# A state-space layer and a gated attention on one core: other places for a few waits, and the last sequence's end in two halves

## The chip, the core and the metric

The kernel runs on one core of a Trainium2 chip, in float32 throughout. A core has TensorE (PE: matmuls and transposes through the identity), VectorE (DVE), ScalarE (ACT), GpSimd (POOL) and SyncE (SP), which issues most of the DMAs; GpSimd issues those that add to memory. The metric is the time of one execution in microseconds (us); lower is better.

## The reference

For each of B=8 sequences of S=512 tokens with D=256 features:

```python
x = x + layernorm(mamba(layernorm(x)))
x = x + layernorm(ffn_block(layernorm(x)))

# mamba: 512 channels, 16 states, convolution of 4 taps
x_ssm, z = split(x @ in_proj_w.T)
xc = silu(conv(x_ssm) + conv_b)
dt_r, Bv, Cv = split(xc @ x_proj_w.T)
dt = softplus(dt_r @ dt_proj_w.T + dt_proj_b)
h[t] = exp(dt * A) * h[t-1] + dt * Bv * xc      # a scan over the tokens
y = sum over states of h * Cv, + xc * D
return (y * silu(z)) @ out_proj_w.T

# ffn_block: 16 heads of 64 features, 8 experts each, 2 of them chosen
q, k = rope(src @ Wq), rope(src @ Wk)
gv, go = top-2 gates, sigmoid(src @ Wsel_v), sigmoid(src @ Wsel_o)
v = sum over experts of gv * (src @ Wv)
o = softmax(q @ k.T / 8) @ v
src = ln(src + sum over heads and experts of (o * go) @ Wo)
return ln(src + relu(src @ W1 + b1) @ W2 + b2)
```

## The kernel before

**Stages.** A sequence b goes through four generators. `front(b)` does layernorm, input projection, convolution and the preparation of dt: ScalarE's Abs, Exp and Ln of `row`, a row of bc_d broadcast to all partitions. `mamba(b)` runs 32 scan steps (four groups of channels by eight pairs of states). A step is, on VectorE, `h = bt * dtx`, a scan with the decays `da` that ScalarE has made one step ahead, and `h * ct`; for sequence 0 the scan reads `ps_u`, made by TensorE. GpSimd's DMAs add the results into `xc` (L566). Then come the gate, the output projection, a norm, a second norm (`xn`), transposes into features (`ps_tr_g`, copied to `xt`) and the logits of the experts (`ps_sel`). `best()` turns logits into the top-2 gates on VectorE (reciprocals, maxima, comparisons; some 0.69 us a row): `best(0)` gives `gv`, the gates of v, and puts the sequence into `state`; `heads(b)` then runs `best(1)` for the gates of the outputs, `gt`, transposes them (`ps_go`, L779), copies them to `go` and stores them in DRAM (`go_d`); then the sequence is in `gated`. `inputs_of[b]` is set as soon as the matmuls of the logits are issued.

**Attention.** The 16 heads go in eight pairs. `Pair.project` makes q and k (`ps_qk`, L810) with weights `wqk` from `wqk_d`, a DRAM copy in which q's weights have been scaled by `later_constants`; `scores` (`ps_s`, L848), a softmax on VectorE and ScalarE, `turn_over` (`ps_pt`, L883), `values` (`ps_v`, L907: all experts; VectorE weighs them, `ve`, and GpSimd sums them into `v`), `attend` (`ps_o`, L937, copied to `o`), `weigh` (`og = o * gb`, where `gb` is a broadcast load from `go_d`, L959) and `add_output` (`ps_a`, L983, summed over all pairs in one bank pair). After a sequence's last pair `feed_forward` adds `xt`, transposes the sum (`ps_acc`, L1012), normalizes, transposes (`ps_tr_f`), applies the two layers (`ps_f`, L1040 and L1062) and two more norms, and stores the result.

**Order.** The order of four engines' instructions is written by hand: `ahead()` interleaves a pair's parts with the sums of the pair before and the projection of the pair after,

```python
for part in (
    "v0", "s0", 0, 1, "v1", "s1", 2, 3, "t0", "s2", "v2", "t1", "s3", following, 4,
    "v3", 5, "t2", 6, "t3", 7,
):
```

where numbers are `add_output(k)` of the pair before and `following` is the projection of the next pair, which for a sequence's last pair is the first of the next sequence. Into this `_Order` mixes everything else by planned costs and due times: a generator yields how long its next part should wait, and that part is issued when TensorE's planned time has come so far (a `Free` wait as soon as due, a plain wait only where VectorE is planned idle). `order_of.run(until)` lets the plan go on until a condition holds. So a changed wait moves instructions in the queues of TensorE, VectorE, ScalarE and GpSimd; each engine then executes its queue in order. SyncE's order is left to the scheduler. All VectorE instructions carry line L175, that of a helper, and are told apart by their tiles.

The mamba of sequence b+1 runs on VectorE, ScalarE and GpSimd beside the attention of sequence b. The last sequence's feed-forward has nothing beside it.

Of the kernel before, what the change touches and what calls it, by code (L numbers as in the profile page):

```python
# [26 lines left out]
F32 = mybir.dt.float32  # L27
AF = mybir.ActivationFunctionType
ALU = mybir.AluOpType
# [3 lines left out]
P = 128  # L33
B, S, D = 8, 512, 256
ND = D // P
NT = S // P
# [3 lines left out]
H, HP, E, F = 16, 64, 8, 1024  # L40
NF = F // P
# [15 lines left out]
NET, FIRST = -9, 0.2  # L57
# [40 lines left out]
class _Order:  # L98
# [11 lines left out]
    def pe(self, us):  # L110
        self.now += us
        self.here = self.now
# [103 lines left out]
def _layers(  # L216
# [3 lines left out]
    nc = tc.nc  # L220
    with ExitStack() as ctx:
        pool = lambda name, bufs, **kw: ctx.enter_context(tc.tile_pool(name=name, bufs=bufs, **kw))
        const = pool("const1", 1)
        wpool = pool("weights", 2)
        seq = pool("seq", 2)
        big = pool("big", 7)
        half = pool("half", 5)
        work = pool("work", 2)
# [37 lines left out]
        def later_constants():  # L266

            nc.sync.dma_start(out=w_sel, in_=wsel)
            nc.sync.dma_start(out=angle[:, :, 0, :], in_=rope)
            half_turn = half.tile([P, P], F32, tag="half", name="half_turn")  # L270
            nc.sync.dma_start(out=half_turn, in_=turn)
            nc.sync.dma_start(out=b1_t, in_=b1)
            nc.sync.dma_start(
                out=rows_t.rearrange("p r d -> p (r d)"),
                in_=rows[:, : 4 * D].to_broadcast([P, 4 * D]),
            )
            yield 8.0


            vector.tensor_reduce(sign, half_turn, AX.X, ALU.add)  # L280
            vector.tensor_scalar(angle[:, 1, 0, :], angle[:, 1, 0, :], sign, None, ALU.mult)

            for i in range(H // 2):
                w = wpool.tile([P, 2, ND, P], F32, tag="wqk", name=f"wqk_s_{i}")
                nc.sync.dma_start(out=w, in_=wqk[i])
                yield 6.0
                while i > 1 and 0 not in state:
                    yield Free(2.0)
                nc.scalar.mul(w[:, 0], w[:, 0], HP**-0.5)
# [25 lines left out]
        def front(b):  # L315
# [127 lines left out]
            nc.sync.dma_start(  # L443
                out=row, in_=bc_d[b][2 * NS : 2 * NS + 1, :].to_broadcast([P, S])
            )
            yield free(1.0)
            if b > 1:
                yield from gate()
            yield free(2.0)
# [4 lines left out]
            for m in range(0, NC, 2):  # L454
                u = tile_for(f"u_{b}_{m}", "og")
                for i in range(2):
                    nc.scalar.activation(u[:, i, :], row, AF.Abs, **step_size(m + i))
                yield free(1.4)
                nc.scalar.activation(u, u, AF.Exp, scale=-1.0)
                us.append(u)  # L460
                yield free(1.1)
            while b == 1 and at["step"] < steps - 1:
                yield Free(0.5)
            for u in us:
# [308 lines left out]
        def heads(b, best, gt):  # L773

            yield from best(1, gt)
            yield Free(1.5)
            ps = banks(f"ps_go_{b}")
            for t in range(NT):
                nc.tensor.transpose(  # L779
                    ps[:, 0, bass.ts(t, P)], gt[:, t].rearrange("p h e -> p (h e)"), ident  # L780
                )
            pe(0.6)
            yield Free(0.05)
            go = half.tile([P, S], F32, tag="half", name=f"go_{b}")
            nc.scalar.copy(go, ps[:, 0, :])
            nc.sync.dma_start(out=go_d[b], in_=go)
            gated.add(b)

        class Pair:
# [3 lines left out]
            def __init__(self, b, pair):  # L793
                self.b, self.pair, self.id = b, pair, f"{b}_{pair}"
                self.xt = inputs_of[b]
                self.p, self.og = {}, {}

                self.done = set()

# [130 lines left out]
            def attend(self):  # L930


                self.need(*((of, t) for of in ("pt", "v") for t in range(NT)))
                po = banks(f"ps_o_{self.id}")
                for t in range(NT):
                    for j in range(2):
                        nc.tensor.matmul(  # L937
                            po[j * HP : j * HP + HP, 0, :], lhsT=self.v[:, j, t, :],
                            rhs=self.pt[:, j, t, :], start=(t == 0), stop=(t == NT - 1),
                        )  # L940
# [12 lines left out]

            def weigh(self, q):

                gb = wpool.tile([P, 2, S], F32, tag="gb", name=f"gb_{self.id}_{q}")
# [7 lines left out]
                og = self.og[q] = work.tile([P, 2, S], F32, tag="og", name=f"og_{self.id}_{q}")  # L964
                vector.tensor_tensor(og, self.o.to_broadcast([P, 2, S]), gb, ALU.mult)

            def add_output(self, k):

                if self.pair == 0 and k == 0:
                    sums[self.b] = psum_a.tile([P, ND, S], F32, tag="sum", name=f"ps_a_{self.b}")  # L970
                pa, q, i = sums[self.b], k // 2, k % 2
                order_of.run(lambda: q in self.og)
                if i == 0:
                    w = self.wo = wpool.tile(
                        [P, 2, D], F32, tag="wo", name=f"wo_{self.id}_{q}"
                    )
# [5 lines left out]
                for c in range(ND):  # L982
                    nc.tensor.matmul(  # L983
                        pa[:, c, :], lhsT=self.wo[:, i, bass.ts(c, P)], rhs=self.og[q][:, i, :],
                        start=(self.pair == 0 and k == 0),
                        stop=(self.pair == H // 2 - 1 and k == E - 1),
                    )
                pe(1.71)
                if i == 1 and q + 2 < E // 2:
                    after(0.05, lambda: self.weigh(q + 2))  # L990

        def feed_forward(b, pa):

# [90 lines left out]
            nc.sync.dma_start(out=out[b].rearrange("(t p) d -> p t d", p=P), in_=z)  # L1084
            finished.add(b)

# [6 lines left out]
        def follow(b, pair):  # L1093

            b, pair = (b, pair + 1) if pair + 1 < H // 2 else (b + 1, 0)
            if b < B:
                order_of.run(lambda: b in (state if b else inputs_of))
                pairs[b, pair] = Pair(b, pair)
                pairs[b, pair].project()

# [13 lines left out]
                    part()  # L1114
                order_of.run()

        last = None
        with tc.manual_schedule(engines=MANUAL):
            first = front(0)
            order_of.start(first, 0, next(first))  # L1120
            order_of.start(mamba(0), 0)
            order_of.start(front(1), FIRST, 9.0)
            first_constants()
            order_of.run(lambda: 0 in scanning)
            order_of.start(later_constants(), NET)
            order_of.run(lambda: 0 in inputs_of)
            pairs = {}
            follow(-1, H // 2 - 1)
            for b in range(B):
# [12 lines left out]
            order_of.run(lambda: not (order_of.queue or order_of.rest))  # L1142


# [81 lines left out]
```

## Time and profile before

| | us |
|---|---|
| three runs | 3694.61, 3695.30, 3702.96 |
| median | 3695.3 |
| profiled execution | 3698.07 |
| its span on the core | 3696.3 |
| busy: TensorE | 3413.1 (92%) |
| busy: VectorE | 3047.2 (82%) |
| busy: ScalarE | 1645.2 (45%) |
| busy: GpSimd | 1681.2 (45%) |

The span runs from the first to the last recorded instruction; 1.8 us of the execution lie around it. The granted clock of TensorE is 0.965 of full speed over the span. In the profile's slices a digit is the busy share in tenths, and PEclk the granted clock in tenths. A timeline row gives start and duration, engine, line, operation, the tiles (out<-in), their shapes and how many instructions of one kind follow each other; the bracket behind it gives the idle time before it on that engine and what ended it. A 512-column matmul appears as two records in the trace. Rows of the largest groups, by TensorE's line: sums `ps_a` 967.1 us, `ps_v` 946.8, `ps_s` 294.2, `ps_pt` 266.7, `ps_o` 248.3.

### The profile page before, as it was taken

The numbers are of one execution on the slowest core, as the hardware profiler recorded it, in microseconds if no ns is written. First come the engines' busy times: TensorE is split into PE (matmuls) and PEld (weight loads), VectorE is DVE, ScalarE is ACT, GpSimd is POOL, SyncE is SP. The second block draws the span as 40 slices with busy tenths as digits, with TensorE's granted clock in tenths as the row PEclk, the third lists the DMA queues.
The fourth block names the chain that finished last, engine by engine and source line by source line (L and its number), as shares of the span: only waits on it lengthen the run. The fifth ranks groups of instructions, "written<-read, shape, count | busy, mean of one in ns | idle before, by whom it ended". The sixth has DMA issues, their size and how long they took to land.

```text
span 3696.3 us, 34548 instructions
## 1 busy us (share of the span) xinstructions
PE 3413.1 (92%) x10956; PEld 1626.4 (44%) x10956; DVE 3047.2 (82%) x3190; ACT 1645.2 (45%) x2798; POOL 1681.2 (45%) x1593
## 2 busy tenths in 40 slices
PE   5768889999999999999999999999999999999996
PEld 3633334444344444444444544434444444445443
DVE  7878998799989898999989998899988998754443
ACT  5524443545543455344544446443653444332331
POOL 1415663354645545454454545355444556232230
PEclk7879999999999999999999999999999999999998
DMA  4937774576866768477755868568765777344431
GB/s 144 196 93 183 174 176 119 149 186 166 195 150 162 179 168 196 121 182 177 199 142 142 201 149 209 138 152 194 183 168 132 179 191 175 99 120 112 111 92 57
DMA packets 285604, 578.48 MB, mean 157 GB/s; under 512 B 37608, under 2 KB 124904, under 8 KB 285424
## 3 DMA queue, kind: packets, MB, share of 16 engines
q1 hardware_dynamic: 204656, 427.33, 40.0%
q0 software_dynamic: 80768, 148.95, 24.1%
q8 instruction: 89, 1.46, 0.2%
q14 instruction: 91, 0.75, 0.1%
HBM read 405.72 MB, written 21.51 MB: 116 GB/s over the span
## 4 chain that ended last, share of the span: by engine, by line
PE 47%; DVE 26%; issue 8%; DMA 7%; ACT 5%; POOL 5%; SPq 0%; DVEq 0%; POOLq 0%; ACTq 0%
PE ps_v L907 14%; PE ps_a L983 12%; DVE h L175 11%; PE ps_qk L810 5%; DMA xc<-h 5%; PE ps_s L848 4%; PE ps_o L937 3%; PE ps_pt L883 3%; DVE ve L175 2%; DVE og L175 2%; DVE low L175 2%; PE ps_f L1040 1%; DVE xs L175 1%; DVE hit L175 1%; POOL ve L923 1%
## 5 line engine op out<-in xcount | busy, mean ns | idle before, releaser
L983 PE MATMUL ps_a<-og,wo 128*128 128x512 f32 x2048 | 967.1, 605 | 32.8 <-DVE og L175 32.5
L907 PE MATMUL ps_v<-wv,xt 128*128 128x512 f32 x2048 | 946.8, 606 | 21.4 <-DVE y L175 13.2
L923 POOL TENSOR_TENSOR ve<-ve 128x512 f32<-128x512 f32 x256 | 425.3, 1661 | 1144.9 <-DVE ve L175 994.7
L863 ACT ACTIVATE p<-ps_s,low 128x512 f32<-128x512 f32 x512 | 347.3, 683 | 723.6 <-DVE low L175 723.1
L566 POOL DMA_DIRECT2D xc<-h x504 | 465.1, 1103 | 384.7 <-DMA xc<-h 174.6
L907 PEld LDWEIGHTS ps_v<-wv,xt 128*128 128x128 f32 x2048 | 385.6, 193 | 544.8 <-issue 484.2
L983 PEld LDWEIGHTS ps_a<-og,wo 128*128 128x128 f32 x2048 | 373.1, 192 | 506.4 <-issue 429.0
L175 DVE TENSOR_TENSOR_SCAN h<-da,h 128x1024 f32<-128x1024 f32 x228 | 541.0, 2373 | 10.2 <-ACT da L503 0.2
L872 ACT ACTIVATE p<-p,total 128x512 f32<-128x512 f32 x512 | 341.5, 714 | 260.8 <-DVE total L175 260.4
L175 DVE TENSOR_TENSOR og<-o,gb 128x1024 f32<-128x1024 f32 x256 | 319.7, 1269 | 130.3 <-ACT o L943 72.4
L175 DVE TENSOR_TENSOR ve<-ps_v,gv 128x1024 f32<-128x1024 f32 x256 | 311.4, 1216 | 126.5 <-PE ps_v L907 99.3
L889 ACT COPY pt<-ps_pt 128x1024 f32<-128x1024 f32 x256 | 256.9, 1005 | 356.5 <-PE ps_pt L883 355.2
L503 ACT ACTIVATE da<-dt,decay 128x511 f32<-128x511 f32 x512 | 339.7, 713 | 104.6 <-DVE h L175 101.8
L175 DVE TENSOR_TENSOR h<-bt,dtx 128x1024 f32<-128x1024 f32 x228 | 321.2, 1409 | 33.7 <-DMA xc<-h 28.6
L175 DVE TENSOR_TENSOR h<-h,ct 128x1024 f32<-128x1024 f32 x256 | 339.1, 1324 | 3.8
L175 DVE TENSOR_REDUCE low<-ps_s 128x2 f32<-128x1024 f32 x256 | 310.4, 1213 | 26.6 <-PE ps_s L848 25.6
L924 POOL TENSOR_TENSOR ve<-ve 128x256 f32<-128x256 f32 x256 | 319.2, 1247 | 20.1
L832 POOL DMA_DIRECT2D qk<-sin x256 | 204.7, 1212 | 264.5 <-DVE qk L175 127.2
L848 PE MATMUL ps_s<-qk 64*128 64x512 f32 x1024 | 294.2, 650 | 23.7 <-ACT p L863 12.8
L883 PEld LDWEIGHTS ps_pt<-ident,p 128*128 128x128 f32 x2048 | 239.5, 141 | 132.0 <-issue 94.8
L937 PE MATMUL ps_o<-pt,v 128*64 128x512 f32 x1024 | 248.3, 611 | 29.0 <-POOL v L925 16.4
L883 PE MATMUL ps_pt<-ident,p 128*128 128x128 f32 x2048 | 266.7, 273 | 7.6 <-ACT p L872 3.3
(134 smaller groups left out, 3340.3 us busy)
## 6 DMA issues: line engine op xcount, KB each, us to landing
gb<-go_d SPq DMA_DIRECT2D x512, 256.0 KB, 4.9
xc<-h POOLq DMA_DIRECT2D x504, 256.0 KB, 5.7
wv<-in_wv_dram SPq DMA_DIRECT2D x128, 512.0 KB, 5.7
wo<-in_wo_dram SPq DMA_DIRECT2D x512, 128.0 KB, 4.0
ct<-bc_d SPq DMA_DIRECT2D x64, 512.0 KB, 5.9
bt<-bc_d SPq DMA_DIRECT2D x57, 512.0 KB, 5.2
wqk<-wqk_d SPq DMA_DIRECT2D x64, 256.0 KB, 2.6
qk<-sin POOLq DMA_DIRECT2D x256, 64.0 KB, 4.7
```

What stands on the lines that cost most here:

```text
L175: return getattr(self.engine, name)(*args, **kw)
L503: nc.scalar.activation(das[k % 2][:, j, 1:S], dt[:, m, 1:S], AF.Exp, scale=decay[:, m, g + j : g + j + 1],)
L566: nc.gpsimd.dma_start(out=xc[:, k % NC, :], in_=hs[k][:, j, :], accum_op=ALU.add)
L848: nc.tensor.matmul(ps[:, j, :], lhsT=self.qk[feats, 0, bass.ts(t, P)], rhs=self.qk[feats, 1, :], start=True, stop=True,)
L863: nc.scalar.activation(p[:, j, :], ps[:, j, :], AF.Exp, bias=low[:, j : j + 1], accum_out=total[:, j : j + 1],)
L872: nc.scalar.mul(p[:, j, :], p[:, j, :], total[:, j : j + 1])
L883: nc.tensor.transpose(pp[:, j, bass.ts(i, P)], self.p[t][:, j, bass.ts(i, P)], ident)
L907: nc.tensor.matmul(ps[:, i, :], lhsT=self.xt[:, c, bass.ts(t + i, P)], rhs=self.wv[:, c, :], start=(c == 0), stop=(c == ND - 1),)
L923: nc.gpsimd.tensor_tensor(ve[:, :, 0:4], ve[:, :, 0:4], ve[:, :, 4:8], ALU.add)
L924: nc.gpsimd.tensor_tensor(ve[:, :, 0:2], ve[:, :, 0:2], ve[:, :, 2:4], ALU.add)
L937: nc.tensor.matmul(po[j * HP : j * HP + HP, 0, :], lhsT=self.v[:, j, t, :], rhs=self.pt[:, j, t, :], start=(t == 0), stop=(t == NT - 1),)
L983: nc.tensor.matmul(pa[:, c, :], lhsT=self.wo[:, i, bass.ts(c, P)], rhs=self.og[q][:, i, :], start=(self.pair == 0 and k == 0), stop=(self. ...
```

## The change

There are six parts.

1. In `front(1)` the waits before ScalarE's Abs and Exp grow from 1.0, 1.4 and 1.1 to 12.0, 3.5 and 3.5, so that these instructions lie among the scan steps of sequence 0.
2. The scaling of q's weights takes a buffer with the tag `w_m` instead of `wqk`, and from the third on waits for sequence 0's `gated` instead of its `state`, now ahead of the load.
3. `heads` waits 4.0 instead of 1.5 before its transposes.
4. `follow` waits for `inputs_of` (logits issued) for every sequence; before, it waited for `state` (gates of v made) for all but sequence 0.
5. In the last sequence the sums `ps_a` are made in two halves of 256 tokens: four matmuls of 256 columns for a k instead of two of 512, and the input `xt` is added by a matmul with the identity instead of on VectorE. The last pair weighs its four `og` at once, with buffers of other tags for the third and fourth.
6. `last_net` takes the place of the last `feed_forward`. Its weights, `x1` and the second bias are loaded from the last sequence's second pair on, into tiles that the mamba no longer uses; then all stages run for one half of the tokens while the other half is a stage behind.

```diff
             for i in range(H // 2):
-                w = wpool.tile([P, 2, ND, P], F32, tag="wqk", name=f"wqk_s_{i}")
+                while i > 1 and 0 not in gated:
+                    yield Free(2.0)
+                w = wpool.tile([P, 2, ND, P], F32, tag="w_m", name=f"wqk_s_{i}")
                 nc.sync.dma_start(out=w, in_=wqk[i])
                 yield 6.0
-                while i > 1 and 0 not in state:
-                    yield Free(2.0)
                 nc.scalar.mul(w[:, 0], w[:, 0], HP**-0.5)
                 nc.sync.dma_start(out=wqk_d[i], in_=w)
...
-            yield free(1.0)
+            yield free(12.0 if b == 1 else 1.0)
...
                     nc.scalar.activation(u[:, i, :], row, AF.Abs, **step_size(m + i))
-                yield free(1.4)
+                yield free(3.5 if b == 1 else 1.4)
                 nc.scalar.activation(u, u, AF.Exp, scale=-1.0)
                 us.append(u)
-                yield free(1.1)
+                yield free(3.5 if b == 1 else 1.1)
...
         def heads(b, best, gt):
 
             yield from best(1, gt)
-            yield Free(1.5)
+            yield Free(4.0)
...
-                for q in range(2):
+                for q in range(E // 2 if self.final else 2):
                     after(0.8 + 0.1 * q, lambda q=q: self.weigh_soon(q))
...
+            def add_half(self, k, g, w):
+                pa = sums[self.b].rearrange("p g (c s) -> p g c s", c=ND)[:, g]
+                if self.pair == 0 and k == 0:
+                    nc.tensor.matmul(
+                        pa, lhsT=ident, rhs=self.xt[:, :, bass.ts(g, S // 2)],
+                        start=True, stop=False,
+                    )
+                    pe(0.86)
+                for c in range(ND):
+                    nc.tensor.matmul(
+                        pa[:, c, :], lhsT=w[:, bass.ts(c, P)],
+                        rhs=self.og[k // 2][:, k % 2, bass.ts(g, S // 2)],
+                        start=False, stop=(self.final and k == E - 1 and c == ND - 1),
+                    )
...
+        def last_net():
+            b = B - 1
+            w_1 = one.tile([P, ND, F], F32, tag="dt", name="w1_last")
+            w_2 = one.tile([P, NF, D], F32, tag="dtx", name="w2_last")
+            w_o = one.tile([P, E // 2, 2, D], F32, tag="xc", name="wo_last")
+            x1 = big.tile([P, NT, D], F32, tag="big", name="x1_last")
...
+            outputs(0, range(E))
+            outputs(1, range(2))
+            nc.scalar.copy(acc[0], pa[:, 0])
+            outputs(1, range(2, 4))
+            to_tokens(0)
+            outputs(1, range(4, E))
+            normed(0, *first)
+            nc.scalar.copy(acc[1], pa[:, 1])
+            features(0)
+            to_tokens(1)
+            hidden(0, 0)
+            normed(1, *first)
+            hidden(0, 4)
+            features(1)
+            for f in range(0, NF, 4):
+                hidden(1, f)
+            for g in range(2):
+                second(g)
...
-                order_of.run(lambda: b in (state if b else inputs_of))
+                order_of.run(lambda: b in inputs_of)
...
+                    if (b, pair) == (B - 1, 1):
+                        next(net)
...
-            for k in range(E):
-                last.add_output(k)
-                order_of.run()
-            order_of.start(feed_forward(B - 1, sums[B - 1]), NET)
-            order_of.run(lambda: not (order_of.queue or order_of.rest))
+            order_of.run(lambda: not order_of.rest)
+            next(net, None)
```

In `last_net`, `outputs` are the last pair's sums of a half, `to_tokens` and `features` the two transposes with their copies, `normed` a norm with the rows behind it, `hidden` four feature groups of the first layer (256 columns each, in one pair of banks, then four Relus), and `second` the second layer of a half with its two norms and its store.

More of the change, by code (lines that the diff above doesn't have):

```diff
@@ L796, in __init__ @@
                 self.p, self.og = {}, {}
+                self.final = b == B - 1 and pair == H // 2 - 1
                 self.done = set()
@@ L954, in weigh @@
             def weigh(self, q):
-                gb = wpool.tile([P, 2, S], F32, tag="gb", name=f"gb_{self.id}_{q}")
+                spare = self.final and q > 1
+                of, tag = (work, "ve") if spare else (wpool, "gb")
+                gb = of.tile([P, 2, S], F32, tag=tag, name=f"gb_{self.id}_{q}")
                 for j in range(2):
@@ L963, in weigh @@
                     )
-                og = self.og[q] = work.tile([P, 2, S], F32, tag="og", name=f"og_{self.id}_{q}")
+                og = self.og[q] = work.tile(
+                    [P, 2, S], F32, tag="p" if spare else "og", name=f"og_{self.id}_{q}"
+                )
                 vector.tensor_tensor(og, self.o.to_broadcast([P, 2, S]), gb, ALU.mult)
@@ L981, in add_output @@
                         )
[L982 to L987, printed above, removed]
+                if self.b == B - 1:
+                    for g in range(2):
+                        self.add_half(k, g, self.wo[:, i])
+                else:
+                    for c in range(ND):
+                        nc.tensor.matmul(
+                            pa[:, c, :], lhsT=self.wo[:, i, bass.ts(c, P)], rhs=self.og[q][:, i, :],
+                            start=(self.pair == 0 and k == 0),
+                            stop=(self.pair == H // 2 - 1 and k == E - 1),
+                        )
                 pe(1.71)
@@ L990, in add_output @@
                     after(0.05, lambda: self.weigh(q + 2))
+            def add_half(self, k, g, w):
[4 more added lines that the diff above has]
+                        start=True, stop=False,
+                    )
+                    pe(0.86)
+                for c in range(ND):
+                    nc.tensor.matmul(
+                        pa[:, c, :], lhsT=w[:, bass.ts(c, P)],
+                        rhs=self.og[k // 2][:, k % 2, bass.ts(g, S // 2)],
+                        start=False, stop=(self.final and k == E - 1 and c == ND - 1),
+                    )
         def feed_forward(b, pa):
@@ L1085, in feed_forward, with outputs, to_tokens, normed @@
             finished.add(b)
+        def last_net():
[4 more added lines that the diff above has]
+            x1 = big.tile([P, NT, D], F32, tag="big", name="x1_last")
+            b2 = half.tile([P, 1, D], F32, tag="half", name="b2_last")
+            for j in range(2):
+                nc.sync.dma_start(
+                    out=w_o[j * HP : j * HP + HP],
+                    in_=wo[H - 2 + j].rearrange("(i p) q d -> p q i d", i=2),
+                )
+            nc.sync.dma_start(out=w_1, in_=w1)
+            nc.sync.dma_start(out=w_2, in_=w2)
+            nc.sync.dma_start(out=x1, in_=x1_d[b])
+            nc.sync.dma_start(out=b2[:, 0, :], in_=rows[:, 4 * D :].to_broadcast([P, D]))
+            yield
+            pa = sums[b].rearrange("p g (c s) -> p g c s", c=ND)
+            half_of = lambda name: [
+                big.tile([P, ND, S // 2], F32, tag="big", name=f"{name}_last_{g}") for g in (0, 1)
+            ]
+            wide = [P, NT // 2, D]
+            rows_of = lambda i: rows_t[:, i : i + 1, :].to_broadcast(wide)
+            acc, y, yt = half_of("acc"), half_of("y"), half_of("yt")
+            hid = one.tile([P, NF, S], F32, tag="pt", name="hid_last")
+            def outputs(g, ks):
+                for k in ks:
+                    order_of.run(lambda: k // 2 in last.og)
+                    last.add_half(k, g, w_o[:, k // 2, k % 2])
+                    pe(0.86)
+                    order_of.run()
+            def to_tokens(g):
+                ps = banks("ps_acc_last")[:, 0, :].rearrange("p (t d) -> p t d", d=D)
+                for t in range(NT // 2):
+                    for c in range(ND):
+                        nc.tensor.transpose(
+                            ps[:, t, bass.ts(c, P)], acc[g][:, c, bass.ts(t, P)], ident
+                        )
+                nc.scalar.copy(y[g], ps)
+            def normed(g, *then):
+                for _ in norm(y[g], [y[g][:, t, :] for t in range(NT // 2)]):
+                    pass
+                for a, op in then:
+                    vector.tensor_tensor(y[g], y[g], a, op)
+            def features(g):
+                ps = banks("ps_tr_f_last")
+                for c in range(ND):
+                    for t in range(NT // 2):
+                        nc.tensor.transpose(
+                            ps[:, c, bass.ts(t, P)], y[g][:, t, bass.ts(c, P)], ident
+                        )
+                nc.scalar.copy(yt[g], ps[:, :, : S // 2])
+                vector.tensor_tensor(y[g], y[g], b2.to_broadcast(wide), ALU.add)
+            def hidden(g, f):
+                ps = banks("ps_f1_last").rearrange("p a (i s) -> p (a i) s", s=S // 2)
+                for i in range(4):
+                    for c in range(ND):
+                        nc.tensor.matmul(
+                            ps[:, i, :], lhsT=w_1[:, c, bass.ts(f + i, P)], rhs=yt[g][:, c, :],
+                            start=(c == 0), stop=(c == ND - 1),
+                        )
+                for i in range(4):
+                    nc.scalar.activation(
+                        hid[:, f + i, bass.ts(g, S // 2)], ps[:, i, :], AF.Relu,
+                        bias=b1_t[:, f + i : f + i + 1],
+                    )
+            def second(g):
+                ps = banks("ps_f2_last")[:, 0, :].rearrange("p (t d) -> p t d", d=D)
+                for t in range(NT // 2):
+                    for f in range(NF):
+                        nc.tensor.matmul(
+                            ps[:, t, :], lhsT=hid[:, f, bass.ts(g * NT // 2 + t, P)],
+                            rhs=w_2[:, f, :], start=(f == 0), stop=(f == NF - 1),
+                        )
+                vector.tensor_tensor(y[g], y[g], ps, ALU.add)
+                normed(g, (rows_of(2), ALU.mult), (rows_of(3), ALU.add))
+                tiles = slice(g * NT // 2, (g + 1) * NT // 2)
+                normed(g, (x1[:, tiles, :], ALU.add))
+                nc.sync.dma_start(
+                    out=out[b].rearrange("(t p) d -> p t d", p=P)[:, tiles, :], in_=y[g]
+                )
+            first = ((rows_of(0), ALU.mult), (rows_of(1), ALU.add))
+            outputs(0, range(E))
[14 more added lines that the diff above has]
+                hidden(1, f)
+            for g in range(2):
+                second(g)
@@ L1115, in ahead @@
                 order_of.run()
-        last = None
+        last, net = None, last_net()
         with tc.manual_schedule(engines=MANUAL):
```

## The prediction

> **What bounds the kernel now.** I read the page's busy shares and slices first, then the costliest groups, then the start, the sequence boundaries and the end in TensorE's and VectorE's timelines, and last the chain of waits through the end.
>
> ```profile
> PE 3413.1 (92%) x10956; PEld 1626.4 (44%) x10956; DVE 3047.2 (82%) x3190; ACT 1645.2 (45%) x2798; POOL 1681.2 (45%) x1593
> PE   5768889999999999999999999999999999999996
> PEclk7879999999999999999999999999999999999998
> ```
>
> TensorE is the bound: 92% busy, and 129.60 of 129.60 us in the window 3445.90 to 3575.50 (three pairs of heads at 43.2 us each). Nothing in such a stretch gets shorter unless TensorE's work does. Time can be won only where TensorE idles or its clock is low: the first 300 us, the last 81 us, and short gaps inside, at the changes from one sequence to the next. Here is sequence 3's, in TensorE's timeline (start, duration, idle before and releaser), then VectorE's rows of the same place:
>
> ```profile
> 1553.87 3.67 PE L937 MATMUL ps_o<-pt,v 128*64 128x512 f32 x6 [5.68 <-POOL v L925]
> 1559.37 1.11 PE L779 MATMUL ps_go<-ident,gt 128*128 128x128 f32 x4 [1.82 <-DVE gt L175]
> 1560.27 4.59 PE L907 MATMUL ps_v<-wv,xt 128*128 128x512 f32 x8
> ```
>
> ```profile
> 1540.88 3.38 DVE L175 RECIPROCAL s<-s 128x128 f32<-128x128 f32 x4
> 1548.89 1.22 DVE L175 TENSOR_TENSOR ve<-ps_v,gv 128x1024 f32<-128x1024 f32 x1
> 1558.62 0.69 DVE L175 TENSOR_TENSOR gt<-gt,hit 128x512 f32<-128x512 f32 x1
> ```
>
> The last ve of sequence 2 stands on VectorE behind reciprocals, sin and qk of sequence 3, so ps_o waits 5.68; ps_go then waits 1.82 for gt. Both stretch what follows: the granted clock is 0.80 in 1545 to 1570, and the rows beside cost 3.67, 1.11 and 4.59 where a place without a wait (287 to 293) has 1.93, 0.66 and 3.60. Loss at b=3: 5.68 + 1.82 + 1.74 + 0.45 + 0.99 = 10.7 us. The same sum gives 9.5 at b=2 and 12.2 at b=5. At b=4 and b=6 only ps_go waits (3.57 and 3.56, with v at 5.3), 5.3 each. Together 43.0; b=1 and b=7 show no such wait.
>
> The end, in the chain of waits (start, us, what):
>
> ```profile
> 3617.23 3.71 PE ps_a L983 x8
> 3621.64 2.84 DMA wo<-in_wo_dram
> 3624.61 7.21 PE ps_a L983 x16
> ...
> 3642.92 1.95 PE ps_tr_f L300 x8
> 3644.89 1.02 ACT yt L1027
> ...
> 3645.96 9.73 PE ps_f L1040 x16
> 3655.69 7.24 PE ps_f L1062 x32
> 3662.93 6.87 PE ps_f L1040 x16
> 3669.79 7.25 PE ps_f L1062 x32
> 3677.07 1.23 DVE y L175
> ```
>
> Everything is serial: from the last attention sum (3615.3) to the end (3696.3) are 81.0 us, with TensorE busy 48.7.
>
> **The change part by part.** The profiled execution took 3698.1 (span 3696.3 and 1.8 around it), 2.8 above the median 3695.3. The sum is made against it; the forecast then takes the 2.8 off.
>
> *Abs and Exp of sequence 1 (L446, L458, L461).* ScalarE waits 3.88 for row and then runs u ops of 1.52, 1.06 and 1.50 ahead of da; the scan at 123.10 waits 3.13 for that da. Spread over some eight scan steps, each u op fits into ScalarE's slack of a step. Two later scans (175.26, 189.65) wait 2.71 and 3.93 for DMA xc<-h, which issues from POOL behind the scans and may give part back. Between 0 and -3.1; I take -2.0.
>
> *Scaled weights.* Pair 1's projection waits for its weights:
>
> ```profile
> 272.26 5.25 PE L810 MATMUL ps_qk<-xt,wqk 128*128 128x512 f32 x8 [5.51 <-DMA wqk<-wqk_d]
> ```
>
> SyncE issues this load only at 269.48, behind loads and stores of the scaled weights, which hold the two buffers of its tag. With a tag of their own, and with the scaling of weights 2 to 7 put behind sequence 0's go, the loads for pairs 0 and 1 stand early in SyncE's order. That removes 5.51, and 5.25 may become 3.63. The scaling moves into pair 1's softmax on ScalarE, with a store and a load of 256 KB for each weight; ScalarE is 45% busy, so I put it at nothing (uncovered, six rows of at most 0.59: 3.5). Between -7.1 and -2; with the next item -3.6.
>
> *Heads later (1.5 to 4.0) for b=0.* The transposes move behind one ps_v, so go, and with it the gb loads that ps_a at 300.27 (idle 6.21) waits for, come up to 3.6 later; ScalarE's copy by some 1.9. I charge 1.9 of the gain above.
>
> *q and k after the logits, heads later, b=2 to 7.* The new order has ve_(b-1)_7_3 ahead of most of the gating's rows, and ps_go 11 to 14 instructions later at b=2 and 3, where gt (1.82 late) is long done. b=2 keeps about 0.5 of 9.5, b=3 about 0.7 of 10.7: -9.0 and -10.0. From b=4 on there is a price. Logits, q and k follow directly on the last scores of the old sequence in TensorE's queue; before, the transposes ps_tr_g stood 12 to 16 instructions ahead of them. Everything of TensorE queues behind them: four v matmul groups, three turn-overs, the sums. At b=5, VectorE has after ps_s_4_7_3: low 1.21, three BN pairs of 0.6, ln_rs 0.18, h times ct 1.32 (which hides POOL's power of 1.05), xn 1.39. That is 5.9, less the 0.3 or so that the first BN has a start: 5.6 of idle at ps_tr_g, 1.1 for the copy xt, and some 1.3 of low clock after it, by b=3's rows. At b=4 only the last xn row, the low and the power are left: 1.5 + 1.1. b=6 is like b=4. Also, go now stands directly before ps_o_b_0, and the first gb of the sequence needs go copied (0.6), stored (2.4), loaded (4.9) and multiplied (1.2), 9.1 to 11 by whether the issues queue (I take 10.6), against ps_o, the ps_a rest, ps_v and ps_s (3.58 + 0.87 + 3.43 + 1.06 = 8.9): 1.7 late. So b=4 keeps 4.3 of 5.3, b=5 9.7 of 12.2, b=6 4.3 of 5.3: -1.0, -2.5, -1.0. All boundaries: -23.5, between 0 (each wait only changes its name) and -37 (b=4 to 6 lose only the 1.7).
>
> *The last sequence's sums by halves.* A 512-column matmul record costs 1.72/4 = 0.430 (ps_a x4), a 256-column one 7.25/32 = 0.2266 (L1062 x32, at full clock). Per k: 8 x 0.2266 - 4 x 0.430 = +0.093. In seven pairs of eight k: +5.2; adding the input by identity, four records of 0.43, +1.7. Pair 7 is in the end's sum. Cost +6.9, in a stretch where TensorE is 100% busy and nothing hides it; at least 1.7.
>
> The Trainium skill speaks against narrower matmuls too, more mildly: "TensorE: Matmul & The Clock Gate", section Back-to-back issue gap, gives each matmul a fixed 2.5 ns beside its columns. By it the halves would cost an estimated 0.6 for 224 further records, not 5.2; the measured row is the better price, being this kernel's shape.
>
> *The end by halves.* Counted from 3615.3 by the rows above: four og in a row to 3620.7, weights already there (the 3.7 for wo gone). Half 0's sums, 32 records of 0.2266, end 3624.5, half 1's with transposes between at 3632.2. Norm 0 (half the BN, power, multiply and add: some 5 on VectorE) is done at 3633.6, so TensorE idles 1.4 where it idled 8.71. First layer of half 0, 7.25, to 3642.0; the second half's features wait 1.6; then 7.25 to 3651.4, twice 7.25 for the second layer to 3665.9. The last chain has half the rows of 3677.07 to 3692.0 but the same two powers: 8.8, to 3674.7; the output's DMA 4.1 (4.3 before, for twice the size). End 3678.8 against 3696.3: -17.5; -14 if the clock stays low (9.73 instead of 6.87 in one of the four groups). The preloads (3.6 MB of weights and inputs, from pair 1 on) have SyncE's queue ahead of gb and wo loads; DMA is 41% busy there, I charge nothing; a queue blocked for a tile would cost each pair a wait like 2.84.
>
> Sum: -2.0 - 3.6 - 23.5 + 6.9 - 17.5 = -39.7. 3698.1 - 39.7 - 2.8 = 3655.6; as the b=4 to 7 waits were read off an order and not off a trace, I put the forecast 2.4 higher: 3658. Ends: -3.1 - 5.2 - 37 + 1.7 - 17.5 = -61 and 0 + 0 + 0 + 6.9 - 14 = -7; they are unlikely all at once, and the likeliest case's own range is 3640 to 3678.
>
> The same page's section What's actually happening says that TensorE's clock halves after an idle window of about 3.4 us. Row 1553.87 (3.67 for 1.93 after 5.68 idle) agrees; at 640.24 a ps_qk took 5.40 for 3.63 after 1.23 idle alone, which does not. By the page, b=4 and b=6 lose no clock and b=5 does, as in the sum.
>
> **The rivals.** *Boundaries trade waits.* If VectorE, 82% busy and with LEAST gaps in its order, brings xn as late as it brought v, the 23.5 vanish: 3658 + 23.5 = 3682. For it: ps_tr_g waited 13.40 at 221.46 (sequence 0). Against: at b=2 and 3 the old order's row is seen to be late for its place only.
> *Boundaries all clear.* If xn is early, b=4 to 6 gain the 13 that separate 37 from 23.5: 3645.
> *Slower: q and k block the queue.* In the old order q and k came after state, when all was there. Now TensorE, in order, stops at ps_tr_g, ps_sel or ps_qk with ps_o, ps_v and ps_a of the old sequence ready behind. It is slower than before by 11 when the waits at b=4 to 7 exceed my values by (37 + 11)/4 = 12 each, nearly the 13.40 of the first sequence: 3706 or more. VectorE's rows before xn (5.9) speak against it.
> *Halves buy nothing.* If narrow matmuls and six powers instead of three eat 10 of the 17.5, the time is 3668, inside the range; that the change does nothing is excluded by the new order.
>
> **How the numbers follow.** Forecast 0.62; boundaries trade waits 0.17; all clear 0.11; slower 0.10. A measurement of this kernel tells 0.3%, 11 us, from no change: 3684 is the border, and half of the trade case lies above it. Faster 0.62 + 0.11 + 0.09 = 0.82, same 0.08, slower 0.10. The range 3637 to 3690 takes in the clear and the trade case and leaves out the slower one and the ends.
>
> **What would show it.** After, ps_qk of pair 1 has no DMA wait; no ps_o near 1120, 1540 and 2390 waits for POOL v over 1 us; ps_tr_g at b=4 to 6 waits 1 to 6; from the last attention sum to the end are some 64 us; ps_a's last-sequence records are 0.2266. I am wrong if ps_tr_g, ps_sel or ps_qk of b=4 to 7 wait 10 or more, if periods from go to go exceed 428, or if a preload stands between gb loads and TensorE's ps_a.

## The result, and the profile after

The changed kernel is slower: 3734.6 us (median of 3732.28, 3733.98, 3735.28 and 3742.39) against 3696.9 for the kernel before in the same session. The ratio is 1.0105, with a 95% interval of 1.0089 to 1.0121. I had forecast 3658, between 3637 and 3690, with 0.82 on faster. The profiled execution is the longest of the four (3742.4, span 3740.2), some 8 us above the median, so that single rows are read from it and totals from the medians.

The page's first lines, with the same columns as before:

```profile
PE 3418.4 (91%) x11248; PEld 1683.5 (45%) x11248; DVE 3049.8 (82%) x3198; ACT 1653.1 (44%) x2816; POOL 1672.5 (45%) x1596
PE   5768889999899999999998999989999899999997
PEclk7878999999999999999999999999999999999999
```

The work is the same (TensorE is busy 5 us longer), and the span grew by 44: the time went into idling, and it went there in the middle (the 8s), not at the ends. The group of the attention sums says where; here it is in the page before and in the page after (busy us and mean ns, then the idle time ahead of it and its releaser):

```profile
L983 PE MATMUL ps_a<-og,wo 128*128 128x512 f32 x2048 | 967.1, 605 | 32.8 <-DVE og L175 32.5
```

```profile
L993 PE MATMUL ps_a<-og,wo 128*128 128x512 f32 x1792 | 855.9, 611 | 82.7 <-DVE og L175 80.7
```

The group before has the last sequence's sums in it as well; even so, after the change 48 us more are spent waiting for og. The place that I had shown, sequence 3's beginning, is clear, as forecast:

```profile
1548.54 3.65 PE L939 MATMUL ps_o<-pt,v 128*64 128x512 f32 x16
1552.12 3.70 PE L909 MATMUL ps_v<-wv,xt 128*128 128x512 f32 x8
...
1576.06 0.66 PE L779 MATMUL ps_go<-ident,gt 128*128 128x128 f32 x4
```

No bracket, no wait: ps_o runs through, and ps_go, a dozen instructions later, finds gt long done. The granted clock in 1545 to 1570 is 1.00 where it was 0.80. Sequence 4's beginning, in TensorE's timeline, shows the price:

```profile
1966.92 0.77 PE L300 MATMUL ps_tr_g<-ident,xn 128*128 128x128 f32 x5 [1.12 <-DVE xn L175]
1968.98 5.28 PE L712 MATMUL ps_sel<-w_sel,xt 128*128 128x256 f32 x16 [1.30 <-ACT xt L705]
...
2033.31 0.60 PE L779 MATMUL ps_go<-ident,gt 128*128 128x128 f32 x4
2033.84 3.65 PE L939 MATMUL ps_o<-pt,v 128*64 128x512 f32 x16
...
2054.50 5.18 PE L993 MATMUL ps_a<-og,wo 128*128 128x512 f32 x8 [11.48 <-DVE og L175]
```

The waits ahead of the logits are the small ones I had counted. The large one is the last: 11.48 at the first sum of the new sequence (7.70 at b=5, 12.25 at b=6), for which I had put 1.7. Followed backwards through ScalarE's, SyncE's and VectorE's timelines:

```profile
2037.54 0.59 ACT L945 COPY o<-ps_o 128x512 f32<-128x512 f32 x1 [4.59 <-PE ps_o L939]
2038.02 0.59 ACT L785 COPY go<-ps_go 128x512 f32<-128x512 f32 x1
```

```profile
2036.51 0.76 SPq L1025 DMA_DIRECT2D w<-in_w_dram  x1
2037.36 1.76 SPq L984 DMA_DIRECT2D wo<-in_wo_dram  x2
2039.17 1.72 SPq L1057 DMA_DIRECT2D b<-in_rows_dram  x1
2040.98 0.69 SPq L786 DMA_DIRECT2D go_d<-go  x1
2048.22 1.75 SPq L963 DMA_DIRECT2D gb<-go_d  x3
```

```profile
2053.22 1.23 DVE L175 TENSOR_TENSOR og<-o,gb 128x1024 f32<-128x1024 f32 x1 [12.46 <-DMA gb<-go_d]
```

ps_go is done at 2033.9. ScalarE copies it at 2038.0, because its queue has the copy of o first and that waits for ps_o. SyncE stores it at 2041.0, behind the loads of w, wo and b. The first gb load is issued 7.2 later, and og can start 5.0 after that: 19.9 us from ps_go's start to og's, where the four rows of TensorE beside it (ps_o to ps_s) cover 9.2. The load's issue waits until the store has landed: at b=6, where the trace holds the landing, the store landed at 2934.89 and the load was issued at 2934.90. In the kernel before, the first gb load of b=4 was issued at 2001.7, 33 us ahead of its og at 2034.9, so that none of this showed.

The end, in the chain of waits, is shorter (the rows up to the second layer):

```profile
3674.03 10.60 PE ps_a L1013 x40
...
3685.29 1.99 PE ps_a L1013 x8
...
3694.21 7.19 PE ps_f_last L1179 x32
...
3703.52 7.17 PE ps_f_last L1179 x32
3710.69 6.92 PE ps_f_last L1193 x32
```

From the last attend (3672.1) to the end (3740.2) are 68.1 us, against 81.0.

### The profile page after: what moved, and what is told of

Same layout as the page of the kernel before. It is cut to its first block, busy times and chain, and to the rows that moved or that the text cites. A ratio compares the mean times of both kernels' runs of the same rounds, so it can differ in the third digit from the quotient of the medians.

```text
span 3740.2 us, 35144 instructions
## 1 busy us (share of the span) xinstructions
PE 3418.4 (91%) x11248; PEld 1683.5 (45%) x11248; DVE 3049.8 (82%) x3198; ACT 1653.1 (44%) x2816; POOL 1672.5 (45%) x1596
## 4 chain that ended last, share of the span: by engine, by line
PE 43%; DVE 26%; DMA 9%; issue 8%; ACT 6%; POOL 5%; SPq 0%; DVEq 0%; POOLq 0%; ACTq 0%
PE ps_v L909 12%; DVE h L175 9%; PE ps_a L993 9%; PE ps_qk L812 5%; DMA xc<-h 5%; PE ps_s L850 3%; DVE og L175 3%; PE ps_o L939 3%; PE ps_a L1013 3%; DVE low L175 3%; DVE ve L175 3%; PE ps_pt L885 2%; DMA gb<-go_d 2%; POOL ve L925 1%; PE ps_out L676 1%
## 5 line engine op out<-in xcount | busy, mean ns | idle before, releaser
L925 POOL TENSOR_TENSOR ve<-ve 128x512 f32<-128x512 f32 x256 | 413.3, 1614 | 1189.7 <-DVE ve L175 1072.5
L993 PE MATMUL ps_a<-og,wo 128*128 128x512 f32 x1792 | 855.9, 611 | 82.7 <-DVE og L175 80.7
L993 PEld LDWEIGHTS ps_a<-og,wo 128*128 128x128 f32 x1792 | 330.0, 194 | 499.5 <-issue 370.0
L812 PE MATMUL ps_qk<-xt,wqk 128*128 128x512 f32 x512 | 240.7, 614 | 16.3 <-DVE ve L175 9.3
```

Of the source, the lines that this page charges most:

```text
L812: nc.tensor.matmul(ps[:, i, :], lhsT=w[:, i, c, :], rhs=self.xt[:, c, :], start=(c == 0), stop=(c == ND - 1),)
L925: nc.gpsimd.tensor_tensor(ve[:, :, 0:4], ve[:, :, 0:4], ve[:, :, 4:8], ALU.add)
L993: nc.tensor.matmul(pa[:, c, :], lhsT=self.wo[:, i, bass.ts(c, P)], rhs=self.og[q][:, i, :], start=(self.pair == 0 and k == 0), stop=(self. ...
```

## The experiments

Two theories stood at first. A: part 4 (q and k wait for logits only) lets all that VectorE does for the next sequence slip back against TensorE's queue, so that go comes too late. B: part 3 (the longer wait of heads) makes go late.

**Part 4 undone**, the rest kept.

```diff
-                order_of.run(lambda: b in inputs_of)
+                order_of.run(lambda: b in (state if b else inputs_of))
```

> The changed kernel with part 4 undone: follow waits for state again, for all but sequence 0; heads keep 4.0. Theory A (the place of q and k, part 4, lets everything that VectorE does for the next sequence slip about 17 instructions back in TensorE's queue; go, its store and the gb loads then come too late): the waits of 11.5, 7.7, 12.3 and 5 us before ps_a at b=4 to 7 go, ps_tr_g waits no longer at the end of a sequence, and what stays is the start (-6) and the end (-13) against before's 3697: 3678, or down to 3670 if one place more for ps_go also takes its 1.8 to 3.6 us waits for gt away. Theory B (the longer wait of heads makes go late): only ps_tr_g's waits of some 3, 7 and 3 and their low clock go: 3715 to 3722.

3681.6 us, ratio to before 0.9964 (0.9951 to 0.9977). As A said: one condition in the planner's loop is worth 53 us. The waits for og at the first sums of b=4 to 6 are gone. (The 5 us that the expectation puts at b=7 stand inside sequence 6, at 3109 in the changed kernel's trace.)

**Part 3 undone**, the rest kept.

```diff
             yield from best(1, gt)
-            yield Free(4.0)
+            yield Free(1.5)
```

> The changed kernel with part 3 undone: heads wait 1.5 again; ps_go then stands 2 instructions ahead of where the change has it at b=4 to 7, b=3 4 ahead. Theory A: each of the four late go comes some 2.6 us earlier on TensorE and its copy perhaps 4 us earlier on ScalarE (in front of the o copy): -4 to -6 a boundary, 3735 - 20 = 3715 (3708 to 3725). Theory B: the 37 us of og waits at b=4 to 7 go nearly whole: 3690 to 3700.

3734.8 us, 1.0112 (1.0095 to 1.0129): no difference to the changed kernel. B falls. A's size of 20 us falls too: in the trace the waits for og at b=4 to 6 are shorter (8.9, 4.9 and 6.7, in sum by 11), but there are new ones, of 4.0 for og at b=3 and of 10.3 for pt in sequence 2.

**Part 4 alone**, in the kernel before.

> The kernel before with part 4 alone. Theory A: it makes nearly the whole loss: 3735 + 6 (start) + 13 (end) - 20 (go two instructions earlier, as above) = 3734, between 3725 and 3755. Theory B: q and k behind the logits alone cost only ps_tr_g's waits and save the waits for v: 3690 to 3705.

3750.0 us, 1.015 (1.0135 to 1.0165): A's number. Part 4 by itself makes the whole loss.

**Parts 3 and 4 undone**, which leaves start and end.

> The changed kernel with parts 3 and 4 undone: what is left is the start (1, 2) and the end by halves (5, 6). Both theories: 3697 - 6 - 13 = 3678 (3672 to 3684), with before's waits at b=2 to 6 as they were. If the start's 6 us are given back later, as sequence 1's part of the trace hints (its pairs 1 to 7 take 5 us longer), 3684.

3676.8 us, 0.9955 (0.9941 to 0.9968). Start and end together bring 16.6 us (0.0045 of 3697).

**The chain shortened.** The changed kernel with go copied directly behind its transposes, and stored from ScalarE's DMA queue:

```diff
             pe(0.6)
-            yield Free(0.05)
             go = half.tile([P, S], F32, tag="half", name=f"go_{b}")
             nc.scalar.copy(go, ps[:, 0, :])
-            nc.sync.dma_start(out=go_d[b], in_=go)
+            nc.scalar.dma_start(out=go_d[b], in_=go)
```

> The changed kernel (3735) with two edits in heads: ScalarE's copy of go is placed directly behind the transposes (ahead of the copy of o, which waits for ps_o), and its store is issued from ScalarE's DMA queue, not from SyncE's, where at b=4 it came behind loads of w, wo and the bias. TensorE's order stays as in the changed kernel. Theory A1 (the chain go, store, gb, og is what costs most at b=4 to 6): 4.1 for the copy and 1 to 2.4 for the issue come off each of the waits of 11.5, 7.7 and 12.3: -15 to -20, 3715 to 3720. Theory A2 (the waits behind ps_tr_g and the low clock carry it, and the chain's wait is only a part that moves elsewhere, as the heads' 1.5 made it 2 to 6 shorter without a change in time): 3728 to 3736.

3727.6 us, 1.0077 (1.0062 to 1.0092): 7 us better by the medians, less than A1 and near A2. Its ScalarE and SyncE rows tell why A1 was too high:

```profile
2033.14 0.58 ACT L784 COPY go<-ps_go 128x512 f32<-128x512 f32 x1 [0.99 <-PE ps_go L779]
2033.75 0.33 ACTq L785 DMA_DIRECT2D go_d<-go  x1
```

```profile
2041.81 1.78 SPq L962 DMA_DIRECT2D gb<-go_d  x3
```

Counted from ps_go, the store is issued 6.4 us earlier, but the gb issue then comes 8.1 behind it, and og 7.8 behind that, so that og gains 2.8. The store and the gb loads run among the loads of bt, ct, w and wo (the DMA engines are busy 0.78 of the time in 2030 to 2060 of the changed kernel, 0.38 in 1980 to 1996); that this crowd is what makes them slow is likely, but no run isolates it. The three waits fell to 8.7, 6.4 and 8.7, in sum by 7.6, about the time gained.

**The chain cut.** The changed kernel in its own order, where the first pair's gb loads of b=4 to 7 read the stored gates of the sequence before (so that pair's gates are another sequence's):

```diff
-                        in_=go_d[self.b][r : r + 2, :]
+                        in_=go_d[self.b - (self.b > 3 and self.pair == 0)][r : r + 2, :]
```

> The changed kernel (3735), its order untouched, with one operand replaced: at b=4 to 7 the first pair's gb loads read the go_d of the sequence before (long stored), so that nothing there waits for go (the output gates of that pair are those of another sequence). If the chain go, store, gb, og is the cost that I had put at 1.7 a boundary: the waits of ps_a at the second pair of b=4 to 6 (11.5, 7.7, 12.3) fall to 0 to 3, with 1 to 3 us of low clock behind each: -30 to -36, 3699 to 3705. If other late work (tr_g's wait, acc, the norm of the feed-forward) only takes the place: 3720 to 3735.

3699.3 us, 1.0019 (1.0007 to 1.0031): 35 us below the changed kernel, as the theory had it. TensorE at sequence 4's beginning:

```profile
2018.74 0.60 PE L779 MATMUL ps_go<-ident,gt 128*128 128x128 f32 x4
2019.28 3.65 PE L939 MATMUL ps_o<-pt,v 128*64 128x512 f32 x16
...
2028.38 3.70 PE L993 MATMUL ps_a<-og,wo 128*128 128x512 f32 x8
```

The sum follows without a bracket. So 35 of the 58 us between the changed kernel and the one with start and end alone are this chain (by the ratios, 32 of 55). The other 23 are not. The edit does one thing more: with nothing to wait for, SyncE issues the first gb load at 1990.7, 28 us ahead of ps_go, so that these loads leave the crowded place as well.

**The plan's wait behind q and k.** The changed kernel, with the wait for the gates put directly behind the projection:

```diff
                 pairs[b, pair].project()
+                order_of.run(lambda: b in state or not b)
```

> The changed kernel with one line more: follow projects q and k as soon as the logits are issued, and then the planner waits for state, before any further part of the pair (before, it waited ahead of the projection; in the changed kernel it waits only behind the next sequence's first v). q and k are still ahead of the gates in VectorE's order. Theory A (what counts is the place in TensorE's order at which the plan waits for VectorE): the loss goes, ps_tr_g stands 12 instructions ahead of the last scores again, 3672 to 3682. Rival C (q and k ahead of the gates' rows delay gv, gt and go on VectorE): 3715 to 3735.

3732.1 us, 1.0097 (1.0078 to 1.0116). My theory of the place of the wait falls here. ps_tr_g and ps_go are back where they were and wait no more, and the time is lost elsewhere: from the last ps_o of sequence 2 to that of sequence 5, ps_o waits 18.3 for ScalarE's pt (6.1 in the kernel before), 15.2 for POOL v (5.7), and ps_a 15.6 for og (0.7). Rival C's range held, but its mechanism is not shown: ps_go has no wait, and the v that is late is the old sequence's last. What is shown is that the planner's order, once shifted, puts other late work on the path.

**The gates of the outputs later**, in the kernel without part 4, by a planned wait ahead of them (6.0 in the first run, 10.0 in the second):

```diff
+            yield 10.0
             yield from best(1, gt)
             yield Free(4.0)
```

> The first experiment's kernel (changed kernel without part 4, 3680) with a planned wait of 6.0 ahead of the gates of the outputs, so that three of the eight reciprocal rows stand ahead of the old sequence's last ve and the rest behind it; ps_go 16 instead of 19 to 20 instructions ahead of the next ps_o. If the waits of ps_o for POOL v (4.3, 5.7, 5.7 at b=2, 3, 5) come from these reciprocals, they go with some 1.7 to 3 us of low clock each: -15 to -22, 3658 to 3665. If ve waits for sin and qk, or v for GpSimd, 3676 to 3682.

3704.3 us, 1.0018 (1.0008 to 1.0027): slower than without it, and outside what I expected. At each of b=3 to 6 ps_o waits for POOL v (5.29), and in each of sequences 3 to 5 for pt (4.61): the same pattern as in the run before, here without q and k being moved.

> As the one before with 10.0 instead of 6.0: all reciprocals of the outputs' gates stand behind the last ve; ps_go 14 instructions ahead of the next ps_o. Same theory: 3656 to 3665, the waits for POOL v gone, unless go is now late for the gb loads, which the first ps_a of the second pair would show.

3672.4 us, 0.9927 (0.9912 to 0.9942). With all reciprocals behind the last ve the waits for POOL v are gone (0.8 us in three sequences), but a wait of 3.9 at ps_pt and one of 6 at ps_o have come.

**10.0 with part 3 undone as well.**

> The fastest so far (late gates 10.0, 3672) with the heads' wait at 1.5: ps_go stands 15 instead of 14 instructions ahead of the next ps_o, the first sequence's and the second's orders change somewhat. If the order's pattern from b=3 on is what decides, the time stays, 3668 to 3676. If it falls back into the pattern of the planned wait of 6.0 (ps_o behind ScalarE's pt by 4.6 and behind POOL v by 5.3 at each of b=3 to 6), 3695 to 3707.

3697.7 us, 1.001 (0.9998 to 1.0022), a miss, for a reason that I had not thought of: against the run before it loses 25 us by the end of sequence 1 (18 of them in sequence 0) and then nothing up to the end: the pattern from b=3 on stayed, as expected, and the first two sequences' order paid.

**10.0 for sequences 0 to 2 alone.**

```diff
+            yield 10.0 if b <= 2 else 0.0
```

> The kernel of the first experiment (changed kernel without part 4) with the planned wait of 10.0 ahead of the outputs' gates for sequences 0 to 2 alone. TensorE's order is that of the run with 10.0 everywhere up to sequence 2, which at the end of sequence 2 was 13 us ahead of the kernel with start and end alone, and has ps_tr_g 12 and 16 instructions ahead of the last scores in turn from b=3 on, as the kernel before has it, with 426 us a sequence. If a sequence's time from b=3 on is that of its order, the 13 us are kept: 3677 - 13 = 3664 (3658 to 3670). If b=3 pays for it, 3672 to 3678.

3668.5 us, 0.9919 (0.9904 to 0.9934), within the expected range: the fastest version here by the median (the interval overlaps that of 10.0 everywhere), 0.8% ahead of the kernel before and 66 us ahead of the changed one. The 13 us were not all made: by the end of sequence 2 it is 8 us ahead of the run with start and end alone, and a wait of 5.68 for POOL v still stands there; these 8 it keeps (8.6 at the last attend).

**The end alone** (parts 5 and 6 in the kernel before).

> The kernel before with parts 5 and 6 alone (sums of the last sequence and its end by halves). By the trace of the changed kernel the end takes 68.1 instead of 81.0 us after the last attention sum, and the sums by halves cost 0.1 us a pair and 1.8 once: -13 + 2.5 = -10.5, 3684 (3680 to 3688). By my sum for it, -17.5 + 6.9 = -10.6: the same total from other terms. The start (1, 2) is then what the run with start and end has beyond this one: -6, or nothing if it is given back.

3687.6 us, 0.997 (0.996 to 0.9981): 11.1 us of gain, so that the start is worth the remaining 5.5 of 16.6. With some 4 to 5 us of uncertainty in each, that difference is not clear of zero, and no run has the start alone.

## Why the prediction was wrong

**Start: the mechanism was right, the size is not shown.** ps_qk of pair 1 no longer waits for its weights (it runs at 266.87 in 3.70, before at 272.26 in 5.25), and the first sums wait 7.95 for og instead of 6.21, by 1.7 more where I had charged 1.9. I had -5.6 for both items; the difference of the two runs, -5.5, is as near as it is partly by luck, since it is uncertain by some 6.

**End: right in sum, by two errors that cancel.** I had -17.5 and +6.9; measured are -12.9 and +3.1 (from the last ps_o of sequence 6 to that of sequence 7, 371.5 us before and 374.6 in the run with the end alone). The end lost two steps of my chain: half 0's sums ran at a granted clock of 0.84 (3674.0 to 3684.6), though the wait ahead of them was the 1.9 that the kernel before has too, where the clock was 1.00 (3617 to 3632); and VectorE did half 0's last norms until 3726.4, so that half 1's, ready at 3724.5, began 1.9 late. The halves' price came from a misread row. In the last sequence a k takes 1.73 from start to start at 256 columns and 1.72 at 512. The 0.2266 of L1062 is a mean over a row of 32 records (3655.5 to 3662.8) in which four early ones are spaced by 0.26 to 0.32; the other 28 follow each other in 0.216, as the halves do. The rule that I had set aside, the 2.5 ns a matmul of the Trainium skill's "TensorE: Matmul & The Clock Gate", section Back-to-back issue gap, gave an estimated 0.6 for the seven pairs. The five pairs that can be compared took 0.4 longer, 43.29 instead of 43.21 each: the page was nearer than my row. The rest of the 3.1 lies in the sequence's first pairs, with the four records that add the input (2.1) and the preloads.

**The boundaries: this step failed.** By the ends of ps_o, from the end of a sequence's pair 2 to that of the next sequence's (us):

| sequence | 2 | 3 | 4 | 5 | 6 | 7 |
|---|---|---|---|---|---|---|
| before | 449.9 | 426.7 | 430.0 | 426.8 | 426.3 | 394.3 |
| after | 439.2 | 428.7 | 447.1 | 446.7 | 440.6 | 403.2 |
| chain cut | 439.1 | 422.0 | 437.3 | 436.3 | 431.1 | 401.6 |
| change forecast | -9.0 | -10.0 | -1.0 | -2.5 | -1.0 | 0 |
| change measured | -10.7 | +2.0 | +17.1 | +19.9 | +14.2 | +8.9 |

The profiled run of the changed kernel is a long one: at b=3 it has the same program as the run with the chain cut, and 6.7 us more, so that single columns are good to some 7 us. At b=2 the gain came, at b=3 about half of it at best. The waits at ps_tr_g and for xt were what I had worked out: 5.68 and 1.10 at b=5 (forecast 5.6 and 1.1), 3.0 at b=4 (2.6). Two things were wrong.

First, the term "1.7 late" for go, 5 us in sum for b=4 to 6. I had 0.6 + 2.4 + 4.9 + 1.2, rows of an unhurried place, taken as 10.6 against 8.9; at b=4 it was 20.5 against 9.2. In the new order the copy stood behind that of o (+4.1), the store behind loads on SyncE (+2.4), and the next load's issue came 7.2 behind the store's where I had 2.4. Those DMAs were in the order that I had read the 1.7 from; I had asked how long each link takes, and not what stands ahead of it on its queue. This is some 35 us by the medians (31 by the table's columns 4 to 7). The kernel before could have warned me: sequence 0 has the store and the load 2.1 us apart,

```profile
292.24 0.33 SPq L786 DMA_DIRECT2D go_d<-go  x1
...
294.31 9.27 SPq L959 DMA_DIRECT2D gb<-go_d  x8
```

but its table of DMAs, in which the last number is the median time from issue to landing, has more for the same store (of the eight landings two are recorded, 6.5 at b=1 and 4.3 at b=2, and 5.4 is their middle):

```profile
go_d<-go SPq DMA_DIRECT2D x8, 256.0 KB, 5.4
```

The Trainium skill's page "DMA: Bandwidth & Descriptors", section Queues, rings and completion order, says that SyncE's and ScalarE's queues are rings on the same 16 DMA engines, and that on an engine a ring's descriptors are consumed in order; the run with the store on ScalarE's queue agrees with the first part, since with a queue of its own the store still kept the load waiting for 8.1, 6.1 and 5.7 us at b=4 to 6 (7.2, 6.6 and 8.6 on SyncE's), not for 2.1. The second part no run here shows.

Second, I treated the wins and costs as if everything between the boundaries stayed. It did not: in the run with the chain cut, TensorE still idles 63 us from the last ps_o of sequence 2 to that of sequence 5, against 44 in the kernel with start and end alone, and its busy time there is 7 us longer. Some 8 of the 19 are the waits at ps_tr_g and ps_sel, which I had counted; the rest are new ones inside the sequences, less old ones that went, among them 2.7 to 3.5 for og three times, and 6.2 for pt in column 4 of the table. In column 7, where I had forecast nothing, 5.25 of the 8.9 us are one wait for og inside sequence 6 (5.59 in the run with the chain cut, none in the kernel before). My rival "boundaries trade waits" named such a trade, but only for xn, and priced it at the gain. The rival that q and k block the queue had the right sign and the wrong mechanism: the block is at ps_a, behind go, not at ps_tr_g. Of my signs of being wrong, the waits of 10 or more at ps_tr_g, ps_sel or ps_qk did not come; the periods from go to go above 428 did (446.8 and 439.4 from b=4 to 6).

**What stays open** is why the planner's order falls into one pattern or another. Moving q and k with the chain cut or with the wait behind them, or delaying the gates by 6.0, gives some 431 to 439 us a sequence in columns 4 to 6; delaying them by 10.0 gives 428 to 429; the order before has 426 to 430. No experiment here isolates the step of the planner that decides it.

## What to carry to other kernels

When a step moves to just ahead of its use, follow the whole way from it to the use (copy, store, landing, load, product), and for each link look at what stands ahead of it on that queue in the new order. A latency row from a place where the DMA queues are quiet was here a lower bound (2.1 us, and 6.6 to 8.6 where it mattered). Where a planner makes the order, a moved wait is a new order: price the places that change, then leave room on both sides for those that you did not look at, and test one condition at a time, since here one line of six parts was the whole loss.

## What was not expected of the hardware

A 256-column float32 matmul record costs half a 512-column one to within 1% (0.216 against 0.429 us from start to start), though every record has its own weight load. The granted clock fell to 0.84 behind a wait of 1.9 us in the changed kernel's end and stayed at 1.00 behind the same wait in the kernel before. From the issue of go's 256 KB store to the issue of the load that needs it there were 2.1 us in sequence 0 of the kernel before (292.24 to 294.31), and 6.6 to 8.6 at b=4 to 6 of the changed one, among the loads of the next scan and of the feed-forward.
